# Layer 0's weighing with the values loaded and the turned probabilities streamed, four heads in four column strips

## The chip, the cores and the metric

The kernel runs on one core of one Trainium2 chip. The metric is the device time of one execution in microseconds (us). In the profiles PE is TensorE's matmuls, PEld its weight loads, DVE is VectorE, ACT ScalarE, POOL GpSimd. A float32 matmul leaves two MATMUL records and two LDWEIGHTS records in the trace (L260 before: 16,384 of each for 8,192 matmuls), a transpose one of each (L254: 8,192 for 8,192); "record" below means one of these. "Granted clock" is the share of TensorE's full clock that the throttle let through. Every clock interval in the traces of the kernel before (390 of them) and of the changed kernel (220) is at 1.00 or 0.50, so a mean of 0.777 says that 45% of the time was at half.

**Work** = span times mean granted clock, about the time that TensorE would have needed at full clock (its few idle microseconds are in it too).

## The reference, cut to what matters

```python
# x: (16, 1024, 256) float32; adj: (16, 1024, 1024) int32; 8 heads of 32
e = einsum('whqd,whkd->whqk', q, k); e = where(e >= 0, e, 0.2 * e)
attn = softmax(where(adj[:, None] > 0, e, NEG), axis=-1)
h = einsum('whqk,whkd->whqd', attn, v)                  # the weighing: what the change rewrites
out = layernorm(h) ; out = concat([out, x]) @ Wffn.T ; x = layernorm(out) + x      # layer 0
# layer 1: two graph attentions whose scores are a sum of one number per row and one per column,
# then a two-layer feed-forward part with two layer norms
```

## The kernel before

Per batch there are 8 row tiles of 128 queries and 8 heads. For a head, the scores (128 queries by 1,024 keys) are made with 32 rows of the array, the masks are added by another product, VectorE and ScalarE make probabilities of them, TensorE turns these in eight 128x128 pieces, and eight products weigh the values. Layer 1 of the batch before is slotted in between the heads.

```python
def scores(b, t, h, st):
    ...                                      # rows = the head's 32 rows of qT and kT
    nc.tensor.matmul(ps[:, cols], qT[rows, c, t * P:(t + 1) * P], kT[rows, c, cols], ...)      # L234
    nc.tensor.matmul(ps[:, cols], neg_ident, masks[b, t][:, cols], start=False, stop=True)     # L238
    ...                                      # softmax_rows
def weigh(b, t, h, st, p):
    ...                                      # eight transposes (L254), two copies by ScalarE (L255)
    for k in range(NT):                      # pT loaded: 128 columns; v streamed: 32 columns
        nc.tensor.matmul(po[:, h * DH:(h + 1) * DH], pT[:, k, :], v[:, k, h * DH:(h + 1) * DH],
                         start=(k == 0), stop=(k == NT - 1))                                   # L260
def attend(...):                             # layer 1: scores of two rows, left = (1, second), right = (first, 1)
    ...
    nc.tensor.matmul(ps[:, cols], left[:, j * P:(j + 1) * P], right[:, cols], ...)             # L325
```

## Time and profile before

| | |
|---|---|
| time, median of 4 | 11,521.95 us (11,510.14 to 11,528.57) |
| TensorE busy | 99% of the span |
| mean granted clock | 0.777, so work 0.777 x 11,526 = 8,956 us |
| L260, the weighing | 2,558 us busy |
| L234, the scores, 32 rows | 2,794 us busy |
| L325, layer 1's scores, 2 rows | 864 us busy |

The prediction below shows the page's lines for this. One thing that it tells without lines is the third window, 3104 to 3190 us, a weight stage of layer 1. These are the answers for the window as a whole and for L325 in it; after the window's ends come its length, then the busy time (number of instructions) of each engine, then the granted clock:

```profile
3104.00:3190.00 86.00, 86.00 (x262) 49.88 (x262) 35.52 (x69) 22.72 (x38) 8.24 (x10) 0.52 0.04 13
```
```profile
3104.00:3190.00 86.00, 25.36 (x28) 7.67 (x28) 0.52 0.04 13
```

TensorE is busy for all 86 us, yet at about half clock. A busy share of 99% hides that.

### The profile page before, as it was taken

How to read it: one execution, taken by the hardware profiler on the slowest of the kernel's cores; microseconds unless marked ns; L12 is line 12 of the kernel's file. 1: busy time of each engine (PE TensorE's matmuls, PEld its weight loads, DVE VectorE, ACT ScalarE, POOL GpSimd, SP SyncE). 2: the span in 40 equal slices, each digit the busy share in tenths (PEclk: the TensorE clock that was granted, in tenths of full speed). 3: DMA queues.
4: the chain of work that ended last, by engine and by line, in shares of the span. 5: the costliest groups of instructions: out<-in, count | busy, mean ns of one | idle time of the engine just before them, and what ended most of it. 6: DMA issues, size and time to landing. Idle time of an engine off the chain costs nothing.

```text
span 11526.0 us, 108885 instructions
## 1 busy us (share of the span) xinstructions
PE 11425.8 (99%) x44576; PEld 7020.6 (61%) x44576; DVE 4517.5 (39%) x8531; ACT 2991.9 (26%) x5185; POOL 1407.3 (12%) x2311
## 2 busy tenths in 40 slices
PE   8999999999999999999999999999999999999999
PEld 5666656566565665656656566665666656566565
DVE  3234334343343433434344343433434334343343
ACT  2222222222222222222222222222222222222221
POOL 0001102011020110201011010110101102011022
PEclk6568879687796876978778786787868879687798
DMA  1000000000000000000000000000000000000000
GB/s 59 0 1 15 8 1 23 0 15 8 1 23 0 15 8 6 17 1 17 6 15 8 1 17 6 15 8 1 17 6 15 8 1 19 4 10 8 1 4 4
DMA packets 59090, 112.49 MB, mean 10 GB/s; under 512 B 5728, under 2 KB 41696, under 8 KB 58592
## 3 DMA queue, kind: packets, MB, share of 16 engines
q1 hardware_dynamic: 58592, 105.54, 2.8%
q8 instruction: 351, 5.75, 0.2%
q14 instruction: 147, 1.20, 0.0%
HBM read 88.75 MB, written 16.78 MB: 9 GB/s over the span
## 4 chain that ended last, share of the span: by engine, by line
PE 86%; POOL 2%; DVE 2%; issue 0%; ACT 0%; POOLq 0%; DVEq 0%; ACTq 0%
PE ps_s L234 19%; PE ps_a L260 18%; PE ps_t L254 9%; PE ps_s L325 7%; PE ps_s L238 5%; PE ps_a L378 4%; PE ps_a L388 4%; PE ps_a L346 4%; PE ps_a L360 3%; PE ps_a L223 3%; PE ps_a L313 2%; PE ps_a L211 2%; PE ps_s L327 2%; PE ps_a L285 1%; PE ps_a L288 1%; POOL rs L166 1%
## 5 line engine op out<-in xcount | busy, mean ns | idle before, releaser
L260 PEld LDWEIGHTS ps_a<-v,pT 128*128 128x128 f32 x16384 | 2504.3, 238 | 745.0 <-issue 434.1
L234 PE MATMUL ps_s<-kT,qT 32*128 32x512 f32 x4096 | 2793.7, 796 | 1.2 <-DVE nshift L155 1.2
L260 PE MATMUL ps_a<-v,pT 128*128 128x32 f32 x16384 | 2558.2, 316 | 0.6 <-ACT pT L255 0.2
L255 ACT COPY pT<-ps_t 128x512 f32<-128x512 f32 x2048 | 1148.0, 587 | 4856.0 <-PE ps_t L254 4855.4
L151 DVE TENSOR_SCALAR_CACHE_REDUCE p<-ps_s 128x1024 f32<-128x1024 f32 x1024 | 1252.6, 1223 | 2268.2 <-PE ps_s L238 2251.4
L254 PEld LDWEIGHTS ps_t<-ident,p 128*128 128x128 f32 x8192 | 1313.2, 180 | 322.4 <-issue 196.8
L254 PE MATMUL ps_t<-ident,p 128*128 128x128 f32 x8192 | 1475.2, 336 | 0.1
L234 PEld LDWEIGHTS ps_s<-kT,qT 32*128 32x128 f32 x4096 | 811.5, 228 | 950.2 <-issue 879.7
L156 ACT ACTIVATE p<-p,nshift 128x1024 f32<-128x1024 f32 x1024 | 1175.9, 1148 | 809.6 <-DVE nshift L155 809.6
L152 DVE SCALAR_TENSOR_TENSOR p<-p,ps_s 128x1024 f32<-128x1024 f32 x1024 | 1247.8, 1219 | 29.3
L325 PE MATMUL ps_s<-right,left 2*128 2x512 f32 x1024 | 863.6, 976 | 3.3 <-DVE left L315 2.0
L165 POOL TENSOR_SCALAR rs<-mv 128x1 f32<-128x1 f32 x512 | 118.8, 232 | 6068.4 <-DVE mv L163 5614.5
L238 PE MATMUL ps_s<-mask,neg_ident 128*128 128x512 fp8e4 x2048 | 809.0, 484 | 0.0
L238 PEld LDWEIGHTS <-neg_ident 128*128 128x128 bf16 x2048 | 136.8, 102 | 1010.3 <-issue 998.6
L151 DVE TENSOR_SCALAR_CACHE_REDUCE att<-ps_s 128x1024 f32<-128x1024 f32 x256 | 313.5, 1225 | 921.7 <-PE ps_s L327 921.7
L332 POOL TENSOR_SCALAR wh<-wh,gden 128x256 f32<-128x256 f32 x256 | 238.4, 931 | 3363.2 <-DVE nshift L155 3122.8
L156 ACT ACTIVATE att<-att,nshift 128x1024 f32<-128x1024 f32 x256 | 294.1, 1149 | 1050.0 <-DVE nshift L155 1050.0
L378 PE MATMUL ps_a<-rT,wf 128*128 128x512 f32 x1024 | 558.5, 647 | 5.6 <-DVE y L167 5.6
L388 PE MATMUL ps_a<-wf,hid 128*128 128x256 f32 x2048 | 495.1, 393 | 20.0 <-DVE y L167 20.0
L360 PE MATMUL ps_a<-wh,att 128*128 128x256 f32 x2048 | 490.8, 387 | 0.1
L346 PE MATMUL ps_a<-att,wh 128*128 128x512 f32 x1024 | 480.6, 617 | 0.0
L388 PEld LDWEIGHTS ps_a<-wf,hid 128*128 128x128 f32 x2048 | 387.7, 196 | 102.1 <-DVE y L167 28.9
(99 smaller groups left out, 7417.4 us busy)
## 6 DMA issues: line engine op xcount, KB each, us to landing
adj_i<-in_adj_dram SPq DMA_DIRECT2D x128, 512.0 KB, 3.3
xs<-in_x_dram SPq DMA_DIRECT2D x16, 1024.0 KB, 5.4
out_dram<-xs SPq DMA_DIRECT2D x32, 512.0 KB, 2.9
wf<-in_L_gnn_w_ff_dram SPq DMA_DIRECT2D x2, 1024.0 KB, 9.6
w<-in_L_gnn_W_dram SPq DMA_DIRECT2D x2, 256.0 KB, 6.6
wf<-in_L_gnn_Wffn_dram SPq DMA_DIRECT2D x1, 512.0 KB, 7.9
wq<-in_L_gnn_Wq_dram SPq DMA_DIRECT2D x1, 256.0 KB, 6.1
wk<-in_L_gnn_Wk_dram SPq DMA_DIRECT2D x1, 256.0 KB, 6.2
```

What stands on the lines that cost most here:

```text
L151: nc.vector.tensor_scalar(p, ps, -1.0, None, op0=OP.mult, op1=OP.min, accum_out=nmax)
L152: nc.vector.scalar_tensor_tensor(p, p, -ALPHA, ps, op0=OP.mult, op1=OP.max)
L156: nc.scalar.activation(p, p, AF.Exp, bias=nshift, scale=1.0, accum_out=den)
L234: nc.tensor.matmul(ps[:, cols], qT[rows, c, t * P:(t + 1) * P], kT[rows, c, cols], start=True, stop=False)
L238: nc.tensor.matmul(ps[:, cols], neg_ident, masks[b, t][:, cols], start=False, stop=True)
L254: nc.tensor.transpose(pt[:, i * P:(i + 1) * P], p[:, k * P:(k + 1) * P], ident)
L255: nc.scalar.copy(pT[:, kh * TPH:(kh + 1) * TPH, :].rearrange("p c q -> p (c q)"), pt)
L260: nc.tensor.matmul(po[:, h * DH:(h + 1) * DH], pT[:, k, :], v[:, k, h * DH:(h + 1) * DH], start=(k == 0), stop=(k == NT - 1))
L325: nc.tensor.matmul(ps[:, cols], left[:, j * P:(j + 1) * P], right[:, cols], start=True, stop=False)
L346: nc.tensor.matmul(pa, wh[:, j, fc * P:(fc + 1) * P], big[:, j, cols], start=(j == 0), stop=(j == NT - 1))
L378: nc.tensor.matmul(pa, wf1[:, dc, hc * P:(hc + 1) * P], rT[:, dc, cols], start=(dc == 0), stop=(dc == DC - 1))
L388: nc.tensor.matmul(pa[:, :D], hid[:, hc, t * P:(t + 1) * P], wf2[:, hc, :], start=(hc == 0), stop=(hc == HC - 1))
```

## The change

The operands of the weighing change places. Before, the turned probabilities are the loaded operand (128 columns) and 32 columns of values stream. After, 32 columns of values are loaded and 128 columns of turned probabilities stream; the output has 32 rows, and the four heads of a group write to four 32-partition strips of one accumulator. A record then uses 32 of the array's columns. "Strip" and "column strip" below go by the partitions that the program names. The result comes out turned, so that it is copied and transposed back. To have four heads at hand, their turned probabilities wait in four buffers; memory for them is found elsewhere.

```diff
-    def weigh(b, t, h, st, p):
-        v = st[4]
-        pT = sb.tile([P, NT, P], FT, tag="pT", name="pT", bufs=2)
+    def turn(b, t, h, p):
+        pT = sb.tile([P, NT, P], FT, tag="pT", name="pT", bufs=4)
         ...
+        turned[h] = pT
+    def weigh(b, t, c, st):
+        ...
         for k in range(NT):
-            nc.tensor.matmul(po[:, h * DH:(h + 1) * DH], pT[:, k, :], v[:, k, h * DH:(h + 1) * DH],
-                             start=(k == 0), stop=(k == NT - 1))
+            for r in range(HPC):
+                h = c * HPC + r
+                nc.tensor.matmul(po[r * DH:(r + 1) * DH, c * P:(c + 1) * P], v[:, k, h * DH:(h + 1) * DH],
+                                 pTs[r][:, k, :], start=(k == 0), stop=(k == NT - 1))
     def after_heads(b, t, st):
+        oT = sb.tile([P, DC, P], FT, tag="hnT", name="oT")
+        nc.vector.tensor_copy(oT.rearrange("p c q -> p (c q)"), po[:, :D])
         ...
+        for c in range(DC):
+            nc.tensor.transpose(pt[:, c * P:(c + 1) * P], oT[:, c, :], ident)
 ...                          # order: weigh a group of four just before the next group's first head is turned
-            ti = sb.tile([P, N], I32, tag="adj", name="adj_i", bufs=2)
+            ti = sb.tile([P, N], I32, tag="adj", name="adj_i", bufs=1)
-        left = sb.tile([2, N], FT, tag="left", name="left")
+                left = sb.tile([2, HALF], FT, tag="left", name="left")     # made twice, half each time
 ...                          # small pool 4 -> 3 buffers; y shares hn's place; comments cut
```

More of the change, by code (lines that the diff above doesn't have):

```diff
@@ L50, in tile_gnn_layers @@
     sb = ctx.enter_context(tc.tile_pool(name="sb", bufs=1))
-    small = ctx.enter_context(tc.tile_pool(name="small", bufs=4))
+    small = ctx.enter_context(tc.tile_pool(name="small", bufs=3))
     psum = ctx.enter_context(tc.tile_pool(name="psum", bufs=2, space=bass.MemoryType.PSUM))
@@ L103, in tile_gnn_layers @@
     load_adj(0, 0)
-    load_adj(0, 1)
     g1c, b1c = load_cols(g1, "g1c"), load_cols(b1, "b1c")
@@ L128, in tile_gnn_layers @@
                               allow_slow_non_contiguous=True)
-        wT = sb.tile([P, DC, D], FT, tag="pT", name="wT", bufs=2)
+        wT = sb.tile([P, DC, D], FT, tag="pT", name="wT", bufs=4)
         for fc in range(DC):
@@ L245, in tile_gnn_layers @@
     dens, heads_out = {}, {}
-    def weigh(b, t, h, st, p):
-        v = st[4]
-        pT = sb.tile([P, NT, P], FT, tag="pT", name="pT", bufs=2)
+    turned = {}
+    def turn(b, t, h, p):
+        pT = sb.tile([P, NT, P], FT, tag="pT", name="pT", bufs=4)
         for kh in range(NH):
@@ L255, in weigh @@
             nc.scalar.copy(pT[:, kh * TPH:(kh + 1) * TPH, :].rearrange("p c q -> p (c q)"), pt)
-        if h == 0:
+        turned[h] = pT
+    def weigh(b, t, c, st):
+        v = st[4]
+        if c == 0:
             heads_out[b, t] = ps_acc()
         po = heads_out[b, t]
+        pTs = [turned.pop(c * HPC + r) for r in range(HPC)]
         for k in range(NT):
-            nc.tensor.matmul(po[:, h * DH:(h + 1) * DH], pT[:, k, :], v[:, k, h * DH:(h + 1) * DH],
-                             start=(k == 0), stop=(k == NT - 1))
+            for r in range(HPC):
+                h = c * HPC + r
+                nc.tensor.matmul(po[r * DH:(r + 1) * DH, c * P:(c + 1) * P], v[:, k, h * DH:(h + 1) * DH],
+                                 pTs[r][:, k, :], start=(k == 0), stop=(k == NT - 1))
     def after_heads(b, t, st):
@@ L266, in after_heads @@
         po = heads_out.pop((b, t))
+        oT = sb.tile([P, DC, P], FT, tag="hnT", name="oT")
+        nc.vector.tensor_copy(oT.rearrange("p c q -> p (c q)"), po[:, :D])
         rden = small.tile([P, H], FT, name="rden")
         nc.vector.reciprocal(rden, dens.pop((b, t)))
+        yield
+        pt = ps_trans()
+        for c in range(DC):
+            nc.tensor.transpose(pt[:, c * P:(c + 1) * P], oT[:, c, :], ident)
         hn = sb.tile([P, D], FT, tag="hn", name="hn")
         nc.vector.tensor_tensor(hn.rearrange("p (h d) -> p h d", h=H),
-                                po[:, :D].rearrange("p (h d) -> p h d", h=H),
+                                pt[:, :D].rearrange("p (h d) -> p h d", h=H),
                                 rden[:, :, None].to_broadcast([P, H, DH]), op=OP.mult)
@@ L288, in after_heads @@
             nc.tensor.matmul(pa[:, :D], hT[:, dc, :], wffnT[:, dc, :], start=False, stop=(dc == DC - 1))
-        y = sb.tile([P, D], FT, tag="y", name="y")
+        y = sb.tile([P, D], FT, tag="hn", name="y")
         normalize(y, pa[:, :D])
@@ L302, in attend, with two_rows @@
     def attend(b, srcT, w, wa, big, wh):
-        left = sb.tile([2, N], FT, tag="left", name="left")
         right = sb.tile([2, N], FT, tag="right", name="right")
+        def two_rows(dst, cols, o, one):
+            pa = ps_acc()
+            for dc in range(DC):
+                nc.tensor.matmul(pa[:2, :], wa[:, dc, o:o + 2], srcT[:, dc, cols],
+                                 start=(dc == 0), stop=(dc == DC - 1))
+            nc.vector.tensor_scalar(dst, pa[:2, :], ident[:2, one:one + 1], None, op0=OP.add)
         for nh in range(NH):
             cols = slice(nh * HALF, (nh + 1) * HALF)
-            for dst, o, one in ((right, 0, 1), (left, 2, 0)):
-                pa = ps_acc()
-                for dc in range(DC):
-                    nc.tensor.matmul(pa[:2, :], wa[:, dc, o:o + 2], srcT[:, dc, cols],
-                                     start=(dc == 0), stop=(dc == DC - 1))
-                nc.vector.tensor_scalar(dst[:, cols], pa[:2, :], ident[:2, one:one + 1], None, op0=OP.add)
+            two_rows(right[:, cols], cols, 0, 1)
             yield
@@ L321, in attend @@
         for j in range(NT):
+            if j % TPH == 0:
+                left = sb.tile([2, HALF], FT, tag="left", name="left")
+                two_rows(left, slice(j * P, j * P + HALF), 2, 0)
             ps = ps_scores()
@@ L324, in attend @@
                 cols = slice(nh * HALF, (nh + 1) * HALF)
-                nc.tensor.matmul(ps[:, cols], left[:, j * P:(j + 1) * P], right[:, cols], start=True, stop=False)
+                nc.tensor.matmul(ps[:, cols], left[:, (j % TPH) * P:(j % TPH + 1) * P], right[:, cols],
+                                 start=True, stop=False)
             for i in range(NT):
@@ L414, in tile_gnn_layers @@
     make_mask(0, 0)
+    load_adj(0, 1)
     state = project(0)
@@ L417, in tile_gnn_layers @@
         units = [(t, h) for t in range(NT) for h in range(H)]
-        probs = {}
+        probs, ready = {}, deque()
         for u in range(-AHEAD, len(units)):
@@ L422, in tile_gnn_layers @@
                 if h == 0:
+                    make_mask(*divmod(b * NT + t + 1, NT))
                     load_adj(*divmod(b * NT + t + 2, NT))
-                    make_mask(*divmod(b * NT + t + 1, NT))
                 probs[t, h] = scores(b, t, h, state)
@@ L428, in tile_gnn_layers @@
             t, h = units[u]
-            weigh(b, t, h, state, probs.pop((t, h)))
-            if h == H - 1:
-                posts.append(after_heads(b, t, state))
+            if h % HPC == 0 and ready:
+                wt, wc = ready.popleft()
+                weigh(b, wt, wc, state)
+                if wc == DC - 1:
+                    posts.append(after_heads(b, wt, state))
+            turn(b, t, h, probs.pop((t, h)))
+            if h % HPC == HPC - 1:
+                ready.append((t, h // HPC))
             step(posts, 1)
@@ L436, in tile_gnn_layers @@
                 xs_of[b + 1] = load_x(b + 1)
+        while ready:
+            wt, wc = ready.popleft()
+            weigh(b, wt, wc, state)
+            posts.append(after_heads(b, wt, state))
         assert not layers
```

## The prediction

The 850 us of four strips are 600, a quarter of 2,400, and 250 for weight loads, the author's estimate. What the trace before shows of a weight load, at full clock: 190 to 192 ns for one of 128 columns (L346, L260) and 83 for one of 2 (L313), so 107 ns for 126 columns. A "visit to another mode" is a group of 32-row or two-row records among 128-row ones.

> **What bounds the kernel now.** I read the busy shares first, then the clock row, then the chain of waits, then the groups by line, and last the order of time on TensorE inside two windows.
>
> ```profile
> span 11526.0 us, 108885 instructions
> PE 11425.8 (99%) x44576; PEld 7020.6 (61%) x44576; DVE 4517.5 (39%) x8531; ACT 2991.9 (26%) x5185; POOL 1407.3 (12%) x2311
> ...
> PEclk6568879687796876978778786787868879687798
> ...
> PE 86%; POOL 2%; DVE 2%; issue 0%; ACT 0%; POOLq 0%; DVEq 0%; ACTq 0%
> ...
> L260 PEld LDWEIGHTS ps_a<-v,pT 128*128 128x128 f32 x16384 | 2504.3, 238 | 745.0 <-issue 434.1
> L234 PE MATMUL ps_s<-kT,qT 32*128 32x512 f32 x4096 | 2793.7, 796 | 1.2 <-DVE nshift L155 1.2
> L260 PE MATMUL ps_a<-v,pT 128*128 128x32 f32 x16384 | 2558.2, 316 | 0.6 <-ACT pT L255 0.2
> ...
> L254 PE MATMUL ps_t<-ident,p 128*128 128x128 f32 x8192 | 1475.2, 336 | 0.1
> ```
>
> TensorE is busy 99% of the span and the chain of waits is 86% TensorE, so what TensorE is spared comes off the time; VectorE (39%) and ScalarE (26%) are far from binding. L260 is the line that the change rewrites: 16,384 records for 8,192 matmuls (each float32 matmul leaves two records with a weight load each). Its weight loads (2504 us) fill as much time as its matmuls (2558 us): 128 columns of weights are loaded to stream 32. The order of time, first where the clock is full, then where it is halved:
>
> ```profile
> 3018.49 1.87 PE L260 MATMUL ps_a<-v,pT 128*128 128x32 f32 x16
> 3020.20 2.39 PE L346 MATMUL ps_a<-att,wh 128*128 128x512 f32 x5
> ```
> ```profile
> 309.92 3.62 PE L260 MATMUL ps_a<-v,pT 128*128 128x32 f32 x16
> 313.47 2.07 PE L234 MATMUL ps_s<-kT,qT 32*128 32x512 f32 x2
> ```
>
> One head's 16 records hold the path for 1.71 us at full clock (107 ns each) and for 3.55 us at half. Over all 1,024 heads: a group's mean busy time is 2558.2/1024 = 2.50 us, between 1.87 and 3.62, so about 64% of the heads run at full clock; 1024 x (0.64 x 1.71 + 0.36 x 3.55) gives about 2,430 us of path. I use 2,400 us, 21% of the span.
>
> The clock matters as much. The row shows stretches at 0.5 to 0.6 and others at 0.9, with TensorE equally busy in both. Two windows of TensorE's busy time and granted clock (the column after the x-counts), then the same windows for L260 alone:
>
> ```profile
> 200.00:600.00 400.00, 400.00 (x1270) 252.82 (x1269) 119.40 (x215) 97.83 (x165) 18.79 (x35) 0.54 0.00 0
> 3020.00:3050.00 30.00, 30.00 (x97) 13.97 (x97) 5.91 (x10) 4.77 (x9) 0.00 (x0) 1.00 0.00 0
> ```
> ```profile
> 200.00:600.00 400.00, 131.88 (x640) 128.36 (x640) 0.54 0.00 0
> 3020.00:3050.00 30.00, 2.34 (x21) 2.30 (x21) 1.00 0.00 0
> ```
>
> In the first window (layer 0 of the first batch, alone) L260 holds 131.9 us and L234, by the same query, 151.1: 71% of the time. In the second they hold 2.3 and 4.2 of 30 us, 22%. A third window (3104 to 3190 us: L260, L234 and layer 1's two-row products of L325, together 75%) is granted 0.52. So the clock falls where the array does little per unit of time: L234 uses 32 of 128 rows, L325 two, and L260 streams 32 columns in the 107 ns in which 128 could pass. Few columns do not seem to count: the 128-row, 2-column products of L313 stand in a window (3050 to 3060 us) with a clock of 1.00.
>
> [...] four records of L234 take 1.92 us from first to next start (3045.61 to 3047.53) where 128-row records of the same length take 4 x 0.43 = 1.71, about 0.2 us for a visit to another mode.
>
> **The change part by part.** Removed: L260's 16,384 records, 2,400 us of path. Added: 16,384 records that load 32 columns of v and stream 128 columns of turned probabilities, four heads in four strips, in unbroken runs of 32 matmuls (64 records). A 128x512 record takes 0.43 us at full clock, so 128 columns take 107 ns: as long as the weight load that it replaces. The whole gain therefore hangs on how many strips run at a time:
> - One: 107 ns per record as before; 2,400 us, nothing saved. Loads stay hidden even so, because L313, also narrow, has its two 0.43 us matmuls at that spacing.
> - Two: the two records of one matmul share a strip, so if starts are in order, a strip's second record overlaps only with the next strip's first. 53 ns per record, 1,200 us.
> - Four: 27 ns per record; 600 us, [...] so I put 850.
>
> Added besides: two transposes per row tile to turn the result back, 256 x 1475.2/8192 = 180 ns, 46 us on TensorE. A copy of 128x256 per tile on VectorE (128 x 0.42 us, as the like x1T copy, 54 us), hidden under VectorE's 61% idle time. Mode visits: about 256 runs of the new kind, but by the order of instructions the scores' pairs are split less often; I count 3,653 mode changes before and 3,741 after, 88 more at about 0.1 us, 9 us. Moved: one adjacency buffer instead of two (its transfer is 3.3 us against over 50 us per row tile), `left` in two halves, three small buffers: none on the path. Four probability buffers are held until four heads are turned; the products stand after two more heads' scores, so ScalarE's copies (0.59 us each) should be done.
>
> Sums at unchanged clock: one strip 11,520 + 55 = 11,575; two strips 11,520 - 1,200 + 55 = 10,375; four 11,520 - 1,550 + 55 = 10,025.
>
> Then the clock. The mean is 0.777, so 45% of the span, about 5,140 us, is at half. The new records stream all the time over all 128 rows, and a run of 64 is 3.4 us or more at full clock with two strips at a time[...]: it should lift the clock, and in layer 0 alone only L234 remains of low kind (with two strips, by half-clock times, 4.0 of about 8.4 us per head, 48% instead of 71%). Layer 1's two-row products stay and will still pull it down. 48% lies between the 22% that kept full clock and the 71% that lost it, so I guess that a third of the remaining half-clock time turns full, each microsecond of it saving half. Two strips: the half-clock time left is 5,140 - 650 = 4,490; a third, halved, is 750: 9,625. Four: 4,300 left, 715: 9,310. One: 5,140, 855: 10,720.
>
> **The rivals.** No concurrency of strips in float32 (time near 11,575, or 10,720 with the clock's help): for it, nothing in this trace shows overlap[...]. [...] A new wait: turned buffers or copies could hold TensorE at the runs of 64; against it, ScalarE is 74% idle; it would cost some 1 us x 256, under 3%. An unchanged clock: 10,375 at two strips; layer 1's low-row work, which the change leaves, speaks for it. [...]
>
> **Range and chances.** I give two strips 0.45, four 0.25, one 0.25, and 0.05 to something else. Weighing 9,625, 9,310 and 10,720, and a clock that may move less, I predict 9,700 us; 9,100 to 10,750 should hold it 8 times in 10. Faster by over 2%: 0.93; within 2%: 0.04; slower: 0.03.
>
> **What would show it.** The spacing of the new records in a run of 64: about 107, 53 or 27 ns at full clock tells the case. The mean granted clock should rise from 0.777 to about 0.84, and the window 200 to 600 us should no longer read 0.54. TensorE should stay above 97% busy. Wrong would be a run of 64 that takes over 7 us at full clock, a clock that stays at 0.78, or idle gaps before the runs put down to ScalarE's copies.

## The result, and the profile after

The changed kernel took 8,675.31 us (median of 4, 8,660.73 to 8,681.47); the kernel before 11,521.95 us. The ratio is 0.7529, 95% interval 0.7518 to 0.754. The direction was right and the size was not: 8,675 us lies below the range's lower end of 9,100.

The page after, with the lines that answer to those of before:

```profile
span 8658.9 us, 109659 instructions
PE 8549.5 (99%) x44832; PEld 4639.3 (54%) x44832; DVE 4521.5 (52%) x8659; ACT 2915.0 (34%) x5185; POOL 1394.7 (16%) x2311
...
PEclk9979889798897988979889898897988989889898
...
PE 92%; DVE 3%; POOL 2%; DMA 1%; ACT 1%; issue 1%; SPq 0%; POOLq 0%; ACTq 0%; DVEq 0%
...
L233 PE MATMUL ps_s<-kT,qT 32*128 32x512 f32 x4096 | 2340.3, 690 | 0.0
...
L346 PE MATMUL ps_s<-right,left 2*128 2x512 f32 x1024 | 747.0, 865 | 0.3 <-DVE gden L353 0.3
...
L270 PE MATMUL ps_a<-pT,v 128*32 128x128 f32 x16384 | 624.1, 295 | 11.5 <-DVE y L166 7.4
...
L270 PEld LDWEIGHTS ps_a<-pT,v 128*32 128x32 f32 x16384 | 483.2, 117 | 199.9 <-issue 163.2
```

TensorE is still the bound (99% busy, 92% of the chain of waits). No new wait took the place of the old work: 11.5 us of TensorE's idle time lie before the new products. L270 is the old L260, with the same 16,384 records, and its busy time fell from 2,558 to 624 us. The scores (L233, the old L234) were not touched, and yet lost 453 us (2,794 to 2,340): the clock row shows why, with 7 to 9 where there were 5 to 9. Order of time on TensorE, one run of the new products and what follows it:

```profile
402.45 1.96 PE L270 MATMUL ps_a<-pT,v 128*32 128x128 f32 x64
404.34 0.88 PE L255 MATMUL ps_t<-ident,p 128*128 128x128 f32 x6
```

Sixty-four records in 1.89 us, 29.5 ns each, where 107 would be one at a time: four run together, and by the order of the program these four are of four strips. (195 of the 256 runs are whole in the trace, and each of these takes 1.88 or 1.89 us; the others are split by products of layer 1, so "unbroken" in the prediction was not quite so.) The start times of the single records show it (from the trace, in us):

```
402.454 402.461 402.468 402.474 | 402.588 402.594 402.601 402.608 | 402.697 402.703 402.710 402.717 | ...
```

Four starts lie 7 ns apart, and the next four follow 0.109 us after.

The clock, in the same stretch of both kernels (200 to 350 us, layer 0 of the first batch alone). Before, then after:

```profile
200.00:350.00 150.00, 150.00 (x472) 95.63 (x471) 44.65 (x81) 36.37 (x61) 7.52 (x14) 0.53 0.00 0
```
```profile
200.00:350.00 150.00, 148.60 (x1132) 82.24 (x1132) 98.86 (x183) 80.07 (x144) 15.08 (x28) 1.00 0.01 1
```

With the same engine just as busy, 472 records passed before and 1,132 after; without the weighing (240 and 576 of them), 232 and 556. The mean clock rose from 0.777 to 0.886, and the work fell from 8,956 to 0.886 x 8,658.9 = 7,672 us. At the old clock that work would take 7,672/0.777 = 9,874 us, so of the 2,850 us gained some 1,650 belong to less work and some 1,200 to the clock. The split depends on the order: with the clock first (8,956/0.886 = 10,108 us) it is some 1,450 and 1,420.

### The profile page after: what moved, and what is told of

It is laid out like the page before. It is cut to its first block, busy times and chain, and to the rows that moved or that the text cites. A ratio compares the mean times of both kernels' runs of the same rounds, so it can differ in the third digit from the quotient of the medians.

```text
span 8658.9 us, 109659 instructions
## 1 busy us (share of the span) xinstructions
PE 8549.5 (99%) x44832; PEld 4639.3 (54%) x44832; DVE 4521.5 (52%) x8659; ACT 2915.0 (34%) x5185; POOL 1394.7 (16%) x2311
## 4 chain that ended last, share of the span: by engine, by line
PE 92%; DVE 3%; POOL 2%; DMA 1%; ACT 1%; issue 1%; SPq 0%; POOLq 0%; ACTq 0%; DVEq 0%
PE ps_s L233 25%; PE ps_t L255 11%; PE ps_s L346 8%; PE ps_s L237 7%; PE ps_a L270 6%; PE ps_a L368 5%; PE ps_a L400 5%; PE ps_a L410 5%; PE ps_a L222 4%; PE ps_a L382 3%; PE ps_a L326 3%; PE ps_a L210 3%; PE ps_s L349 2%; PE ps_a L304 1%; PE ps_a L301 1%; DVE p L150 1%
## 5 line engine op out<-in xcount | busy, mean ns | idle before, releaser
L233 PE MATMUL ps_s<-kT,qT 32*128 32x512 f32 x4096 | 2340.3, 690 | 0.0
L233 PEld LDWEIGHTS ps_s<-kT,qT 32*128 32x128 f32 x4096 | 741.7, 203 | 983.3 <-issue 965.0
L255 PE MATMUL ps_t<-ident,p 128*128 128x128 f32 x8192 | 1220.3, 292 | 25.6 <-ACT pT L256 22.9
L255 PEld LDWEIGHTS ps_t<-ident,p 128*128 128x128 f32 x8192 | 1017.0, 151 | 324.0 <-issue 138.5
L346 PE MATMUL ps_s<-right,left 2*128 2x512 f32 x1024 | 747.0, 865 | 0.3 <-DVE gden L353 0.3
L237 PE MATMUL ps_s<-mask,neg_ident 128*128 128x512 fp8e4 x2048 | 701.8, 428 | 0.0
L270 PE MATMUL ps_a<-pT,v 128*32 128x128 f32 x16384 | 624.1, 295 | 11.5 <-DVE y L166 7.4
L270 PEld LDWEIGHTS ps_a<-pT,v 128*32 128x32 f32 x16384 | 483.2, 117 | 199.9 <-issue 163.2
L400 PE MATMUL ps_a<-rT,wf 128*128 128x512 f32 x1024 | 495.1, 596 | 0.0
L368 PE MATMUL ps_a<-att,wh 128*128 128x512 f32 x1024 | 474.7, 616 | 0.0
L382 PEld LDWEIGHTS ps_a<-wh,att 128*128 128x128 f32 x2048 | 390.7, 197 | 73.2 <-DVE xs L384 22.9
```

Source lines behind the costliest of these rows:

```text
L255: nc.tensor.transpose(pt[:, i * P:(i + 1) * P], p[:, k * P:(k + 1) * P], ident)
L270: nc.tensor.matmul(po[r * DH:(r + 1) * DH, c * P:(c + 1) * P], v[:, k, h * DH:(h + 1) * DH], pTs[r][:, k, :], start=(k == 0), stop=(k == N ...
L346: nc.tensor.matmul(ps[:, cols], left[:, (j % TPH) * P:(j % TPH + 1) * P], right[:, cols], start=True, stop=False)
L368: nc.tensor.matmul(pa, wh[:, j, fc * P:(fc + 1) * P], big[:, j, cols], start=(j == 0), stop=(j == NT - 1))
L382: nc.tensor.matmul(pa[:, :D], big[:, j, i * P:(i + 1) * P], wh[:, j, :], start=(j == 0), stop=(j == NT - 1))
L400: nc.tensor.matmul(pa, wf1[:, dc, hc * P:(hc + 1) * P], rT[:, dc, cols], start=(dc == 0), stop=(dc == DC - 1))
```

## The experiments

My theory after the result had two parts. **Overlap**: products in different strips run together. **Clock**: the granted clock follows the rows of the array that an instruction addresses while it streams; neither how many columns are in use nor what the data is matters. Rivals: the overlap alone explains the gain and the clock follows from it; the clock counts the share of the whole array in use; the new order of work lifts the clock; the clock follows switching in the data. All kernels below gave the reference's result except the one marked. Their results in one table (work as defined above, from the profiled run):

| run | time, median us | ratio to before | clock | work, us |
|---|---|---|---|---|
| before | 11,522 | 1 | 0.777 | 8,956 |
| the change | 8,675 | 0.7529 | 0.886 | 7,672 |
| one_strip | 9,660 | 0.8386 | 0.894 | 8,636 |
| two_strips | 8,996 | 0.7809 | 0.886 | 7,975 |
| before_wide (wrong result) | 9,626 | 0.836 | 0.948 | 9,115 |
| old_roles | 11,727 | 1.0183 | 0.745 | 8,739 |
| pad_two_rows | 7,745 | 0.6722 | 0.991 | 7,673 |
| pad_scores | 7,634 | 0.663 | 0.972 | 7,430 |
| pad_both | 7,424 | 0.6445 | 0.996 | 7,397 |
| before_padded | 8,657 | 0.7517 | 0.997 | 8,635 |
| pair_scores | 7,568 | 0.6564 | 0.973 | 7,356 |

### one_strip: the same products, strip after strip

```diff
-        for k in range(NT):
-            for r in range(HPC):
+        for r in range(HPC):
+            for k in range(NT):
```

> The changed kernel with the two loops of the products swapped: all eight products of one strip, then the next strip. Same instructions, same operands, same result; only neighbours in the order now share a strip. If strips overlap only where neighbouring products lie in different strips, a run of 64 records takes about 64 x 107 ns = 6.9 us at full clock instead of 1.84, which is 16384 x 0.078 = 1,280 us more work. What the time then becomes tells the clock's rule. If the clock counts rows that stream, whatever the columns, the mean stays at 0.88 or above: (7,672 + 1,280)/0.89 = 10,050 us. If it counts the share of the array in use, one strip of four is a quarter, like the old products, and the mean falls to about 0.78: 11,450 us. If the hardware finds the overlap whatever the order: 8,675 us, as the changed kernel.

Measured: 9,660 us, clock 0.894. A run of 64 records, and what follows it:

```profile
307.10 5.96 PE L270 MATMUL ps_a<-pT,v 128*32 128x128 f32 x64
312.99 0.77 PE L255 MATMUL ps_t<-ident,p 128*128 128x128 f32 x5
```

With nothing changed but the order, 1.89 us became 5.89: the overlap comes from neighbours in different strips and is worth 984 us of the change's gain. It is less than the 6.9 us that I expected, and the start times say why:

```
... 308.111 308.220 308.329 | 308.438 308.444  308.548 308.578  308.657 308.687  308.766 308.796 | 308.905 309.014 ...
```

In the built program the first strip's eight products (16 records) precede all of the second's. Twelve records start 0.109 us apart; then, four times, two start within one such step; then they are single again. The trace does not name a record's strip. If records of one strip do not overlap, as the twelve single ones 0.109 us apart suggest, the doubled ones are of two strips: the second strip's first four records start beside the first strip's last four. The first strip's last three then start after the second strip has begun, out of the program's order. This is inferred from the spacing. Three boundaries with four doubled records make 52 steps of 0.109 us, 5.67 of the 5.89 us; in the program's order, with one doubled record at each boundary, it would be 61 steps, 6.65 us.

The clock says as much. One strip at a time uses a quarter of the columns, and still 0.894 was granted, slightly more than to the change itself. So by these two runs the number of columns does not count, and the higher clock is no result of the overlap. Without nearly all of the overlap the swap of operands alone took 1,862 us off; the work fell by only 320 us of that.

### two_strips: the case that the prediction thought most likely

```diff
-        for k in range(NT):
-            for r in range(HPC):
+        for k, r in [(k, 2 * g + i) for g in range(HPC // 2) for k in range(NT) for i in range(2)]:
```

> The changed kernel with its products in pairs of strips: strips 0 and 1 alternate through all eight steps, then strips 2 and 3. This is the case that the prediction held most likely. Overlap by neighbours: 54 ns per record, a run of 64 in 3.5 us at full clock, 16384 x 0.0255 = 420 us more work than the changed kernel; with the clock counting streaming rows 8,090/0.89 = 9,090 us. If the clock counts the share of the array, half is in use, a mean near 0.83 and 9,750 us.

Measured: 8,996 us, clock 0.886. A run of 64 lasts 3.22 us, 50 ns a record:

```profile
305.19 3.29 PE L270 MATMUL ps_a<-pT,v 128*32 128x128 f32 x64
308.41 0.44 PE L255 MATMUL ps_t<-ident,p 128*128 128x128 f32 x2
```

One, two and four strips give 92, 50 and 29.5 ns a record, and the granted clock is 0.894, 0.886 and 0.886. The time per record falls with the overlap; the clock stays within 0.008.

### before_wide: more arithmetic in the old roles

```diff
-            nc.tensor.matmul(po[:, h * DH:(h + 1) * DH], pT[:, k, :], v[:, k, h * DH:(h + 1) * DH],
+            r, c = h % HPC, h // HPC
+            nc.tensor.matmul(po[:, r * P:(r + 1) * P], pT[:, k, :], v[:, k, c * P:(c + 1) * P],
```

> The kernel before with every product of probabilities and values streaming 128 columns of the values (four heads' worth) instead of the head's 32, into a 512-wide scratch; three quarters of it is wasted and the result is wrong on purpose. A record was held to 107 to 112 ns by its 128-column weight load, and 128 columns stream in 107 ns, so the work is the same, at most 5% longer; the rows stream all of the time instead of a quarter. If the granted clock follows streaming rows, the mean rises from 0.777 to 0.87 or more and the time falls to about 10,000 to 10,400 us though four times the multiplications are done. If the clock rose in the changed kernel for another reason (fewer microseconds of TensorE work, the new order), this kernel stays at 0.78 and 11,500 us or a little above.

Measured: 9,626 us, clock 0.948, with a wrong result as intended. The kernel before, made to do four times the multiplications in its weighing, became 16% faster. Its clock row and its products:

```profile
PEclk9999899999998999999999999899989999899998
```
```profile
L261 PE MATMUL ps_a<-v,pT 128*128 128x128 f32 x16384 | 2171.1, 287 | 15.8 <-ACT pT L255 15.4
```

Its work is even a little larger than before's (9,115 against 8,956). Neither less work nor the new order nor strips lifted the clock here; the one edit is that 128 columns, 107 ns of them, stream in the 112 ns from one record to the next (the median of L260 before, at full clock) where 32 columns did. The gain beat my range for the same reason that the prediction missed: I took the clock's response for weaker than it is.

### old_roles: the new order with the old products

```diff
-                nc.tensor.matmul(po[r * DH:(r + 1) * DH, c * P:(c + 1) * P], v[:, k, h * DH:(h + 1) * DH],
-                                 pTs[r][:, k, :], start=(k == 0), stop=(k == NT - 1))
+                nc.tensor.matmul(po[:, h * DH:(h + 1) * DH], pTs[r][:, k, :], v[:, k, h * DH:(h + 1) * DH],
+                                 start=(k == 0), stop=(k == NT - 1))
 ...                          # loops swapped, no turning back
```

> The changed kernel's order and buffers (four heads turned, then 64 records in one run, one adjacency buffer, three small ones) with the old products: probabilities loaded, 32 columns of values streamed, result not turned back. It tells whether order and buffers alone do anything. My theory: nothing much, 11,300 to 11,650 us and a clock of 0.76 to 0.79. A rival in which grouping the products is what lifts the clock: 0.85 and 10,500 us.

Measured: 11,727 us, 1.8% slower than before, clock 0.745, just outside what I expected (interval 1.0164 to 1.0201: unclear by the 2% rule, but above 1). The order and the buffers bring no gain: the work fell by 2% and the clock fell by 4%. A likely reading, not tried by a run of its own, is that a run of 64 poorly streaming records, some 6.9 us at full clock (64 x 107 ns), fills a whole window of 3.41 us in the fit worked out below, which holds for this run as well (19 of its 3,424 windows missed).

### pad_two_rows, pad_scores, pad_both: rows of zeros

`pad_two_rows` gives layer 1's two-row operands 126 rows of zeros; `pad_scores` copies a head's 32 query rows into a 128-row operand that is zero elsewhere and streams all rows of the keys; `pad_both` does both. The arithmetic result is the same.

```diff
+    right = const.tile([P, N], FT, name="right");  left = const.tile([P, HALF], FT, name="left")
+    nc.gpsimd.memset(right, 0.0);  nc.gpsimd.memset(left, 0.0)
-            two_rows(right[:, cols], cols, 0, 1)
+            two_rows(right[:2, cols], cols, 0, 1)            # left alike; the products take all 128 rows
```
```diff
+    qz = [...]                                               # four [P, P] operands, zeroed once; two masks fewer make room
+        nc.gpsimd.tensor_copy(z[rows, :], qT[rows, c, t * P:(t + 1) * P])
-            nc.tensor.matmul(ps[:, cols], qT[rows, c, t * P:(t + 1) * P], kT[rows, c, cols],
+            nc.tensor.matmul(ps[:, cols], z, kT[:, c, cols],
```

> The changed kernel with layer 1's two-row operands widened to 128 rows of which 126 hold zeros (set once). The product is the same number for number, a product takes as long with 2 rows as with 128, and about 250 visits to the two-row mode fall away (some 50 us). If the clock counts rows that an instruction addresses while it streams, layer 1's weight stages no longer pull it down: mean 0.93, (7,672 - 50)/0.93 = 8,200 us. If it counts switching in the data (zeros do nothing), the clock stays near 0.886 and only the visits are saved: 8,620 us.

> The changed kernel with a head's 32 query rows copied by GpSimd into a 128-row operand whose other rows are zero, against all 128 rows of the keys: same scores, same time per record, no visits to the 32-row mode (some 1,250 visits of 0.2 us, 250 us). Clock counts addressed rows: mean 0.94, 7,420/0.94 = 7,900 us. Only the visits count: 8,400 us. If the copies (1,024 of about 0.3 us on GpSimd) come late, TensorE waits and the time is above that.

> The changed kernel with both paddings. Nothing of low row use is left; if the rule of addressed, streaming rows is the whole story the clock is 0.98 or more throughout and the time is 7,370/0.985 = 7,480 us. If it stays under 0.93 the rule lacks something.

Measured: 7,745, 7,634 and 7,424 us, with clocks of 0.991, 0.972 and 0.996. The first two beat the times expected (8,200 and 7,900 us): once more the clock answered more than I allowed. `pad_two_rows` is the cleanest case: its work is that of the change within the few microseconds that three digits of the clock resolve (7,673 against 7,672), so that the whole 930 us are clock; the 50 us that I expected from fewer visits to another mode did not show. What the two-row products did to the change's clock and what became of it: first the window 412 to 470 us of the changed kernel (layer 1's weight stage), then L346 alone in it; then a window of the padded kernel, and its L348 alone:

```profile
412.00:470.00 58.00, 58.00 (x210) 24.95 (x209) 29.90 (x56) 17.34 (x31) 5.78 (x7) 0.61 0.00 1
```
```profile
412.00:470.00 58.00, 18.52 (x28) 6.34 (x28) 0.61 0.00 1
```
```profile
380.00:440.00 60.00, 59.20 (x374) 31.69 (x373) 40.23 (x76) 27.95 (x51) 5.79 (x7) 1.00 0.00 1
```
```profile
380.00:440.00 60.00, 13.51 (x28) 4.82 (x28) 1.00 0.00 1
```

The same 28 records of the same product (the first 28 of layer 1 in both), 126 rows of them zero, are granted 1.00 in place of 0.61. So in this pair the rows count that are addressed, not data that switches. A two-row record takes no less time to stream: in the changed kernel at full clock they start 429 ns apart within a group, like those of 128 rows (L368). One rival is left by this pair: the padding also takes away TensorE's visits to another mode, where the first of four two-row records takes 0.10 us longer and the last 0.09 us. `pad_scores` leaves the two-row products in place and reaches 0.972; its work is 240 us below the change's, as the estimate for the visits to the 32-row mode had it. Either cure alone removes most of the half-clock time (1,974 us in the changed kernel, some 150 and 420 with one padding): in the changed kernel most of the clock was lost only where both kinds of low product came together. `pad_both` is the fastest kernel, 0.6445 of before, and correct.

A fit to the traces of all eleven kernels, made after the runs, puts this in numbers; it describes these traces and no more. The granted clock's intervals, the first and the last apart, are multiples of 3.41 us in every trace (before: 388 intervals, the shortest 3.413 us). For each window of 3.41 us, add up the streaming time of the records times their share of the 128 rows (107 ns for 128 float32 columns at full clock, half of that for fp8 and bf16, twice at half clock, from the starts in the kernel before: 429 ns apart for 512 float32 columns, 56 for 128 of bf16 and 226 for 512 of fp8, and 853 and 107 for the first two at half clock; no instant counts for more than all 128), as a share of the window. The next window is at full clock when this share is above 0.375 in a window at full clock, or above 0.75 in one at half: right in 28,772 of 28,935 windows. (Counted again on the traces of the kernel before and the changed kernel alone, it is right in 5,824 of 5,871, where "no switch" misses 604; borders of 0.385 and 0.74 fit these two slightly better, 5,835.) In both states that is the same work, 0.375 x 3.41 = 1.28 us at full clock. With the best borders for each, the share of the whole array in use misses 1,415 windows and TensorE's busy time 1,991, where "no switch" misses 2,170; the fit has 163 misses without any term for visits to a mode, or for what the data is. Between the two shares either clock keeps itself in these traces: the kernel before has a mean share of 0.45 in the window 200 to 600 us and stays near half (0.54), the changed kernel 0.59 from 200 to 350 us and stays at full (1.00).

### before_padded: the paddings without the change

The same two edits on the kernel before.

> The kernel before with both paddings and nothing else. The old products of probabilities and values (a quarter of the time streaming) are then the only low part, about a fifth of the time, below the 22% that kept full clock: clock 0.95, 8,650/0.95 = 9,100 us. So 2,400 us of the 2,850 us that the change brought would come without it, and the change on top (pad_both) would be worth 0.82 instead of 0.75.

Measured: 8,657 us, clock 0.997, ratio 0.7517, against 9,100 us and 0.95 expected. Rows of zeros alone are worth as much as the whole change (8,675). What is then left for the change: `pad_both` against `before_padded`, both at full clock, 7,424/8,657 = 0.858 by the medians (0.82 expected), or 1,233 us. Here is the gain with the clock out of it. The weighing in `before_padded`, then in `pad_both`:

```profile
L269 PE MATMUL ps_a<-v,pT 128*128 128x32 f32 x16384 | 1966.0, 273 | 12.2 <-ACT pT L264 12.2
```
```profile
L279 PE MATMUL ps_a<-pT,v 128*32 128x128 f32 x16384 | 555.9, 275 | 12.6 <-DVE y L173 8.2 <-ACT pT L265 4.4
```

1,410 us less, part of which goes to turning the result back (58.6 us in the changed kernel, L284); the rest of the difference to 1,233 us is not split.

### pair_scores: two row strips for the scores

On `pad_two_rows`, the scores of two heads are issued alternately, so that neighbours lie in two row strips (32 rows of qT and kT each; `32*128` in the trace).

```diff
+        pss = [ps_scores() for _ in heads]                   # both score buffers at once
         for kh in range(NH):
+            for h, ps in zip(heads, pss):
+                ...
+                nc.tensor.matmul(ps[:, cols], qT[rows, c, t * P:(t + 1) * P], kT[rows, c, cols], ...)
```

> pad_two_rows, and besides the scores of two heads issued alternately, so that neighbouring products lie in two row strips (their queries and keys lie in rows 32r to 32r+31); four p buffers and thirteen masks make room. If row strips overlap as column strips do, the 4,096 score records cost 0.22 instead of 0.43 us: 880 us less, about 6,870 us, less what is lost because both score buffers now have to come free together. If that wait eats it, or row strips do not overlap: 7,700 us or more.

Measured: 7,568 us, clock 0.973: between the two expectations, and slower than `pad_both`. Where the pair stayed together, it did overlap:

```profile
2029.75 1.99 PE L240 MATMUL ps_s<-kT,qT 32*128 32x512 f32 x8
2031.66 1.04 PE L246 MATMUL ps_s<-mask,neg_ident 128*128 128x512 fp8e4 x4
```

Eight records in 1.91 us, where the kernel before took 1.92 us for four (3045.61 to 3047.53 in the prediction). But the scheduler often tore the pair apart (two records, other work, then six):

```profile
2004.26 1.12 PE L240 MATMUL ps_s<-kT,qT 32*128 32x512 f32 x2
...
2017.64 1.98 PE L240 MATMUL ps_s<-kT,qT 32*128 32x512 f32 x6
```

Over the whole span the scores' busy time fell from 2,087 to 1,546 us, where half would be 1,043. `pad_two_rows`, then `pair_scores`:

```profile
L237 PE MATMUL ps_s<-kT,qT 32*128 32x512 f32 x4096 | 2086.6, 623 | 0.7 <-DVE nshift L158 0.2
L240 PE MATMUL ps_s<-kT,qT 32*128 32x512 f32 x4096 | 1545.9, 630 | 4.6 <-DVE nshift L158 3.3
```

TensorE's busy share fell to 97% and its idle time rose from 115 to 233 us, of which part waits for VectorE. Half of the scores' time was there to be saved, and 177 us came out. By the table, the work fell by 317 us (7,673 to 7,356), and the lower clock (0.991 to 0.973) gave 140 of them back; why the clock fell, and what the torn pairs alone cost, no run separates.

## Why the prediction was wrong

What bounds the kernel and what the clock counts were right. The step on the order of starts in strips was wrong, and the clock's answer was mis-sized; both erred to the same side. The miss, 9,700 - 8,659 = 1,041 us against the profiled run (1,025 against the median), splits as follows: 390 + 133 + 518.

- **How many strips run at a time** (the prediction: two 0.45, four 0.25, one 0.25, "if starts are in order, a strip's second record overlaps only with the next strip's first"). This step failed. By the spacing in `one_strip`, read as above, a strip's first four records start beside the last four of the strip before, and the change itself has four starts 7 ns apart. Four strips it was, 29.5 ns per record. Weighing the other cases put 9,700 in place of the four-strip sum, 9,310: 390 us of the miss. The 9,700 is not the mean that the prediction's own chances give: (0.45 x 9,625 + 0.25 x 9,310 + 0.25 x 10,720)/0.95 = 9,830 us, and a clock that moves less would put it higher still. That slip of 130 us went towards the result by luck.
- **The size of the four-strip term** (850 us of path, of which some 250 for weight loads, an estimate). L270 took 624 us; the loads added nothing (a step of four records is 0.109 us, as from one record of 128 columns to the next in L255). In work my sum was 10,025 x 0.777 = 7,790 us and the measured work 7,672; at the clock of 0.886 that is 133 us of the miss.
- **The clock** ("I guess that a third of the remaining half-clock time turns full"). This term was the worst. The four-strip sum left 4,300 us at half clock and kept two thirds of it, 2,870; measured were 2 x (1 - 0.886) x 8,658.9 = 1,974, so 54% turned. Its 9,310 us meant a clock of 7,790/9,310 = 0.837; at 0.886 it would have read 8,792: about 518 us of the miss.
- **What the clock counts** was right for these kernels: streaming rows, not columns. `before_wide` (0.777 to 0.948), `one_strip` (0.894) and the paddings (0.991, 0.972) each show it. What I lacked was how much low work the full clock stands, and that it takes less to keep it than to win it back (shares of 0.375 and 0.75 of a window in the fit above). I knew that 22% of low products kept it and 71% lost it, and took a point between for a part of the way. After the change L233 held 66.8 of 150 us in the window 200 to 350 us, 45%, at a clock of 1.00:

```profile
200.00:350.00 150.00, 66.83 (x129) 20.26 (x128) 1.00 0.01 1
```

- **Small parts** held: turning back took 58.6 us (L284) for 46; TensorE stayed at 99%; VectorE went from 39 to 52% and hid its copies; the rival of a new wait came to 11.5 us before the products and 25.6 us before the transposes. The window 200 to 600 us, said to leave 0.54, reads 0.88.
- **The range** was too narrow at its low end: 9,100 us was below the best branch by only 210 us, though the clock's term in that branch was named a guess.

## What to carry to other kernels

Read the granted clock beside the busy share: here TensorE was 99% busy and lost a fifth of its speed (0.777), and rows of zeros, which cost no time to stream (7,673 us of work against 7,672), gave as much as the rewritten product. When a product has few output columns, try loading the narrow operand, streaming the wide one, and putting neighbours in the order into different strips: with the clock near full in both it was worth 8,657 to 7,424 us here, and the order decided how much they overlap (1.89 against 5.89 us for the same 64 records). When a term of a prediction is a guess on a threshold, bracket it with the measured points on both sides and let the range reach both outcomes.
